# A graph-attention layer and a GCN layer on one core: other places for pieces of projections, the checks in layer 1, and the end in written order

## The chip, the core and the metric

The kernel runs on one NeuronCore of a Trainium2 chip. Five engines work in parallel, each on its own queue of instructions: TensorE (PE) multiplies matrices, VectorE (DVE) and ScalarE (ACT) compute elementwise, GpSimd (POOL) multiplies and copies, and SyncE (SP) here only issues DMAs. An engine takes its instructions in the order of its queue and stops at one whose semaphores have not come; whatever stands behind it waits too. The metric is the device time of one execution in microseconds (us).

## The reference

N = 2708 nodes with D = 128 features, H = 8 heads per feature. Layer 0 is an attention in which each of the 128 feature rows is a batch element of its own (the reshape cuts the N x 1024 projection so); layer 1 is a two-fold graph convolution with a dense `adj`:

```python
q = (x @ Wq.T).reshape(d, n, h)            # k, v alike; d = 128, h = 8
a = einsum('dnh,dmh->dnm', q, k) * d**-0.5 + adj + adj
a = softmax(a, axis=2)
x = layernorm(x + einsum('dnm,dmh->dnh', a, v).reshape(n, h*d) @ Wo.T)
lh = adj @ (x @ W2) + b2
e  = adj @ (lh @ W4) + b4 + lh @ res_w.T + res_b
x  = layernorm(x + e)
```

All in float32. The attention has 128 x 2708 x 2708 scores, so nearly all time is there.

## The kernel before, in words

**Startup.** `project_all` forms q, k and v of the first two 128-row chunks of x (L377) and stores them to DRAM. The other 20 chunks are projected in 240 "quarters" (chunk, one of q/k/v, a quarter of the columns) in between the attention's work. A quarter is one PE product (L344), a DVE copy (L346), for q and k two POOL instructions (L359, L360), stores (L364) and the load of the next quarter's weights `wc` (L336). `load_quarter(0)` (L407), which loads the first of these, stands on SP behind the stores of project_all.

**Attention.** The 128 feature rows are taken in 32 groups of 4. For each group, six blocks of 452 queries are worked through (the last 448). The keys are 22 chunks of 128 (the last has 20 rows). A block is nine steps, so there are 32 x 6 x 9 = 1728 steps. A step has two to four pieces; in a piece PE forms two tiles of scores in PSUM (L438) and DVE adds `adj` (L445). At the end of a step ACT takes the exponential of a tile `w` of three without `adj` (L534), which POOL multiplies by the exponential of `adj` (L535, `ecol`), and the exponential of the 4, 6 or 8 tiles `e` (L537). PE then adds the tiles up against the values (`add_up`, L455 to L463), at a block's end DVE copies the sums (`hand_on`, L469), and SP stores them to `os_` (L471). In group 0 `first_exp` (L418) forms the exponentials of `adj` and keeps them in DRAM; its `accum_out` gives their row sums for a check. `look_at_near` (L427) takes minima of the same columns in the last three groups.

**Order.** A planner, `interleave` (L40), writes the order of all this down ahead of time, from a cost for each operation; the engines keep that order. The quarters come in it as "amid": before the step numbers in the list `amid` (L474), so every 6 to 7 steps, up to step 1531. A quarter's further jobs (split, store, load) are issued one at a time at the second piece of the following steps.

**The end of layer 0.** After the attention SP loads seven weights (L544 to L550). `layer0_out` takes 22 chunks of 128 nodes: load `ot` (9 x 128 x 128, the sums with the divisor as the ninth row) and `xt`, two chunks ahead (L587, L589); reciprocal (L595); minimum and maximum of the divisor for a check (L598); multiply (L600); eight transposes on PE (L603), a copy by ACT (L605), the product with Wo (L611), the addition of x and its statistics on DVE (L615). After all chunks the normalisation and x @ W2 follow, four chunks at a time (L629 to L651), and a verdict over all checks (L652 to L667). If a check fails the program computes the attention again in a safer way (`tc.If`); this does not occur with these inputs.

**Layer 1.** Two passes of six column blocks (512 wide, the last 148). In each block 22 column tiles of `adjT` (256 KB each) are loaded by SP into 24 buffers (L679) and multiplied on PE (L680). Pass 1 gives `lhT` and from it `hw` (L691); pass 2 gives `eT` (L697), which is transposed (L700), added to x1 (L702), normalised (L577) and stored to `out` by SP (L705), 128 rows at a time. Layer 1 is not in written order: the framework's scheduler orders its instructions.

Of the kernel before, what the change touches and what calls it, by code (L numbers as in the profile page):

```python
# [18 lines left out]
P = 128  # L19
H = 8  # L20
# [10 lines left out]
NEAR_LOW = 1e-30  # L31
NEAR_HIGH = 1e18
# [110 lines left out]
def graph_attention_gcn(ctx: ExitStack, tc: tile.TileContext, x, xT, adj, adjT, adjP, adjS,  # L143
# [42 lines left out]
    ends = const.tile([P, 2, len(QBS) * len(TWO_EXP)], F32, name="ends")  # L186


    with ExitStack() as s:
# [184 lines left out]
        for n in range(2):  # L374
            load_adj(n)

# [30 lines left out]
        load_quarter(0)  # L407
# [5 lines left out]
        def first_exp(b, m):  # L413

            nw = QBS[b][1]
            t = ecols.tile([P, QB], F32, tag="ecol", name="ecol")
            x = b * len(TWO_EXP) + TWO_EXP.index(m)
            nc.scalar.activation(t[:, :nw], adj_cols[0, b, -1 - m][:, :nw], AF.Exp, scale=2.0,  # L418
                                 accum_out=ends[:, 1, x : x + 1])
            nc.sync.dma_start(near_exp[b, m][:, :nw], t[:, :nw])  # L420
            exp_cols[0, b, m] = t

        def look_at_near(g, b, m):

            x = TWO_EXP.index(m)
            if x % 3 == g - NG + 3:
                nc.vector.tensor_reduce(ends[:, 0, ds(b * len(TWO_EXP) + x, 1)], exp_cols[g, b, m][:, : QBS[b][1]],  # L427
                                        AX.X, ALU.min)
# [45 lines left out]
        amid = [2 + 32 * n // 5 for n in range(len(quarters))]  # L474
# [5 lines left out]
        for what, n, c, beside in interleave(plan, len(steps) // len(plan), NU, amid, bufs=5):  # L480
# [14 lines left out]
            if c == 1 and jobs:  # L495
                jobs.pop(0)()
            if c == 0:
# [34 lines left out]
            if c == len(pieces) - 1:  # L532
                look_at_near(g, b, two)
                nc.scalar.activation(w[:, :, :nw], sp[:, :, :nw], AF.Exp, scale=2.0)  # L534
                nc.gpsimd.tensor_mul(w[:, :, :nw], w[:, :, :nw],  # L535
                                     exp_cols[g, b, two][:, :nw].unsqueeze(1).to_broadcast([P, 3, nw]))
                nc.scalar.activation(e[:, :at, :nw], e[:, :at, :nw], AF.Exp, scale=2.0)  # L537
# [5 lines left out]
    wo = keep.tile([P, H, D], F32, name="wo")  # L543
    nc.sync.dma_start(wo.rearrange("g e f -> g (e f)"), WoT)  # L544
    w2, w4, rw = (keep.tile([P, P], F32, name=f"w{i}") for i in range(3))
    for t, src in ((w2, W2), (w4, W4), (rw, res_wT)):
        nc.sync.dma_start(t, src)
    b2_sb, b4_sb, rb_sb, bias = (keep.tile([P, 1], F32, name=f"b{i}") for i in range(4))
    for t, src in ((b2_sb, b2), (b4_sb, b4), (rb_sb, res_b)):
        nc.sync.dma_start(t, src)  # L550
    nc.vector.tensor_add(bias, b4_sb, rb_sb)

# [8 lines left out]
    reach = keep.tile([P, 2, NM], F32, name="reach")  # L561
    nc.gpsimd.memset(reach, 1.0)
    fine = keep.tile([P, 5], F32, name="fine")
# [6 lines left out]
    def layernorm(to, y, w):  # L570
        mv = stat.tile([P, nc.vector.BN_AGGR_DIM], F32, tag="mv", name="mv")
        statistics(mv[:w], y, w)
        sd = stat.tile([P, 1], F32, tag="sd", name="sd")
        nc.scalar.activation(sd[:w], mv[:w, 1:2], AF.Sqrt, bias=eps[:w])
        rs = stat.tile([P, 1], F32, tag="rs", name="rs")
        nc.vector.reciprocal(rs[:w], sd[:w])
        nc.vector.tensor_scalar(to, y, mv[:w, 0:1], rs[:w], ALU.subtract, ALU.mult)  # L577

    def layer0_out(sb, ps, pa, judge):
# [4 lines left out]
        def load(c):  # L584
            i0, w = MC[c]
            ot = sb.tile([P, H + 1, P], F32, tag="ot", name="ot")
            nc.sync.dma_start(ot[:w], o3[ds(i0, w)])  # L587
            xt = sb.tile([P, D], F32, tag="xt", name="xt")
# [3 lines left out]
        def divide(c):  # L592
# [3 lines left out]
            if judge:  # L596
                for i, op in enumerate((ALU.min, ALU.max)):
                    nc.vector.tensor_reduce(reach[:w, i, c : c + 1], ot[:w, H, :], AX.X, op)  # L598
            on = sb.tile([P, H, P], F32, tag="on", name="on")
            nc.vector.tensor_mul(on[:w], ot[:w, :H, :], rd[:w].unsqueeze(1).to_broadcast([w, H, P]))  # L600
# [16 lines left out]

        load(0)
        load(1)
        for c in range(NM + 2):  # L620
            if c + 2 < NM:
                load(c + 2)
            if c < NM:
                divide(c)
            if 0 <= c - 1 < NM:
                project(c - 1)
            if c >= 2:
                add_x(c - 2)
        sd, rs = (sb.tile([P, NM], F32, tag=n, name=n) for n in ("sds", "rss"))  # L629
        nc.scalar.activation(sd, mvs[:, :, 1], AF.Sqrt, bias=eps)  # L630
        nc.vector.reciprocal(rs, sd)
        for c0 in range(0, NM, 4):
            cs = range(c0, min(c0 + 4, NM))
            px = pa.tile([P, 4, P], F32, tag="px", name="px")
            x1T = sb.tile([P, 4, P], F32, tag="x1T", name="x1T")
            pw = pa.tile([P, 4, P], F32, tag="pw", name="pw")
            for c in cs:
                w = MC[c][1]
                nc.vector.tensor_scalar(x1[:w, c, :], ys[:w, c, :], mvs[:w, c, 0:1], rs[:w, c : c + 1],
                                        ALU.subtract, ALU.mult)  # L640
                nc.tensor.transpose(px[:, c - c0, :w], x1[:w, c, :], ident[:w, :w])

            full = len([c for c in cs if MC[c][1] == P])
            parts = [(0, full, P)] + [(c - c0, 1, MC[c][1]) for c in cs if MC[c][1] < P]
            for i, n, w in parts:
                nc.scalar.copy(x1T[:, ds(i, n), :w], px[:, ds(i, n), :w])
            for c in cs:
                w = MC[c][1]
                nc.tensor.matmul(pw[:w, c - c0, :], x1T[:, c - c0, :w], w2, start=True, stop=True)
            for i, n, w in parts:  # L650
                nc.scalar.copy(xw[:w, ds(c0 + i, n), :], pw[:w, ds(i, n), :])  # L651
        if judge:  # L652
            finite = sb.tile([P, NM * D], F32, tag="finite", name="finite", bufs=1)
            nc.vector.tensor_scalar(finite, ys.rearrange("p c f -> p (c f)"), 0.0, 0.0, ALU.mult, ALU.is_equal)
            nc.vector.tensor_reduce(fine[:, 0:1], finite, AX.X, ALU.min)
            bounds = [(reach[:, 0, :], ALU.min, SUM_LOW, ALU.is_ge), (reach[:, 1, :], ALU.max, SUM_HIGH, ALU.is_le)]
            bounds += [(ends[:, 0, :], ALU.min, NEAR_LOW, ALU.is_ge), (ends[:, 1, :], ALU.max, NEAR_HIGH, ALU.is_le)]
            for i, (a, way, limit, op) in enumerate(bounds):
                end = keep.tile([P, 1], F32, name=f"end{i}")
                nc.vector.tensor_reduce(end, a, AX.X, way)  # L660
                nc.vector.tensor_scalar(fine[:, 1 + i : 2 + i], end, limit, None, op)
            every, ones = (keep.tile([P, 1], F32, name=n) for n in ("every", "ones"))
            nc.vector.tensor_reduce(every, fine, AX.X, ALU.min)
            nc.gpsimd.memset(ones, 1.0)
            pf = pa.tile([P, NB], F32, tag="py", name="pf", bufs=2)
            nc.tensor.matmul(pf[:1, :1], every, ones, start=True, stop=True)
            nc.vector.tensor_copy(n_fine, pf[:1, :1])  # L667

    def layer1(s, cols):
# [4 lines left out]
        def propagate(src, n0, nw, last=None):  # L674

            acc = ps.tile([P, NB], F32, tag="wide", name="acc1")
            for m, (m0, mw) in enumerate(MC):
                t = cols.tile([P, NB], F32, tag="col", name="col1")
                nc.sync.dma_start(t[:mw, :nw], adjT[ds(m0, mw), ds(n0, nw)])  # L679
                nc.tensor.matmul(acc[:, :nw], src[:mw, m, :], t[:mw, :nw], start=(m == 0),  # L680
                                 stop=(last is None and m == NM - 1))
            if last is not None:
# [3 lines left out]
        for n0, nw in NBS:  # L686
            acc = propagate(xw, n0, nw)
            nc.vector.tensor_scalar(lhT[:, ds(n0, nw)], acc[:, :nw], b2_sb, None, ALU.add)
            for i, w in chunks(nw, P):
# [4 lines left out]
        for n0, nw in NBS:  # L694
            acc = propagate(hw, n0, nw, (rw, lhT[:, ds(n0, nw)]))
            eT = sb.tile([P, NB], F32, tag="eT", name="eT")
            nc.vector.tensor_scalar(eT[:, :nw], acc[:, :nw], bias, None, ALU.add)  # L697
            for i, w in chunks(nw, P):
                pe = pa.tile([P, NB], F32, tag="narrow", name="pe")
                nc.tensor.transpose(pe[:w, :D], eT[:, ds(i, w)], ident)  # L700
                y = sb.tile([P, D], F32, tag="y", name="y1")
                nc.vector.tensor_add(y[:w], pe[:w, :D], x1[:w, (n0 + i) // P, :])  # L702
                o = sb.tile([P, D], F32, tag="xo", name="xo")
                layernorm(o[:w], y[:w], w)
                nc.sync.dma_start(out[ds(n0 + i, w), :], o[:w])  # L705

    def rest(judge):
        with ExitStack() as s:
            cols = s.enter_context(tc.tile_pool(name="cols1", bufs=24))
            with ExitStack() as t:  # L710
# [3 lines left out]
                t.enter_context(tc.manual_schedule())  # L714
                layer0_out(sb, ps, pa, judge)
            layer1(s, cols)
# [136 lines left out]
```

## Time and profile before

| what | us |
|---|---|
| median of 3 runs (lowest, highest) | 6884.85 (6881.82, 6886.79) |
| profiled execution, its own time | 6884.26 |
| its span | 6882.5 |
| busy PE / DVE / ACT / POOL | 6655.3 / 6106.7 / 6505.4 / 5789.3 |
| last matmul of the attention ends | 6542.9 |
| first transpose of layer 0's end | 6555.6 |
| PE on layer 1 alone from | 6661.6 |
| last product of pass 2 starts | 6873.9 |

The span is from the first to the last instruction of the profiled execution; its own time has 1.8 us more around it. A busy share is an average over stages with different limits, so the stages have to be read on their own. A wait names what an engine waited for last; a wait of an engine that isn't the bottleneck of its stage costs nothing.

### The profile page before, as it was taken

What the parts mean: (1) busy time and instruction counts of PE and PEld (TensorE: products, weight loads), DVE (VectorE), ACT (ScalarE), POOL (GpSimd) and SP (SyncE); (2) the same over time, 40 slices, a digit from 0 to 9 for tenths busy, and PEclk for the clock granted to TensorE, in tenths of its full rate; (3) what the DMA queues carried; (4) which work ended last, traced back from release to release, by engine and by line L of the source; (5) the groups of instructions that cost most, each with busy time, mean ns of one, the idle gap of its engine ahead of it and who ended that gap; (6) DMA issues with size and microseconds to landing.
All of it is one profiled execution on the core that took longest, in us unless ns stands there. A gap on an engine that the chain in (4) does not pass through costs nothing.

```text
span 6882.5 us, 138849 instructions
## 1 busy us (share of the span) xinstructions
PE 6655.3 (97%) x50666; PEld 2002.7 (29%) x50666; DVE 6106.7 (89%) x6373; ACT 6505.4 (95%) x3659; POOL 5789.3 (84%) x2706
## 2 busy tenths in 40 slices
PE   7999999999999999999999999999999999999979
PEld 2222222222222222222222222222222222222254
DVE  6899999999999999999999999999999999999941
ACT  7999999999999999999999999999999999999910
POOL 5899988989888899998889999889898898888800
PEclk8999999999999999999999999999999999999999
DMA  8888888778888877788887778887788878777667
GB/s 254 261 250 250 249 244 248 243 246 250 249 254 245 239 245 244 246 251 252 246 243 248 244 240 250 242 253 243 248 251 247 249 233 239 243 233 230 193 204 233
DMA packets 1168590, 1674.27 MB, mean 243 GB/s; under 512 B 153982, under 2 KB 1135954, under 8 KB 1163802
## 3 DMA queue, kind: packets, MB, share of 16 engines
q1 hardware_dynamic: 1167642, 1664.50, 79.0%
q8 instruction: 402, 6.59, 0.4%
q14 instruction: 290, 2.38, 0.1%
q10 hardware_dynamic: 256, 0.81, 0.1%
HBM read 1582.90 MB, written 81.80 MB: 242 GB/s over the span
## 4 chain that ended last, share of the span: by engine, by line
PE 58%; DMA 11%; DVE 11%; POOL 6%; issue 5%; ACT 5%; SPq 4%; DVEq 0%; ACTq 0%; POOLq 0%
PE acc L463 29%; PE s L438 18%; DVE e L445 10%; POOL w L535 6%; DMA col<-in_adjP 4%; PE acc L680 3%; DMA two<-in_adjP 3%; ACT e L537 3%; PE p L438 2%; PE acc L455 2%; SPq L287 2%; ACT w L534 2%; DMA ecol<-ne 2%; PE s L344 1%; PE acc L460 1%
## 5 line engine op out<-in xcount | busy, mean ns | idle before, releaser
L535 POOL TENSOR_TENSOR w<-w,ecol 128x1356 f32<-128x1356 f32 (+1 forms) x1728 | 5347.8, 3102 | 696.1 <-ACT w L534 601.6
L445 DVE TENSOR_TENSOR e<-s,col 128x904 f32<-128x904 f32 (+1 forms) x4608 | 4817.2, 1091 | 320.6 <-PE s L438 130.3
L537 ACT ACTIVATE e<-e 128x2712 f32<-128x2712 f32 (+5 forms) x1728 | 4593.8, 2658 | 9.3 <-DVE e L445 4.3
L463 PE MATMUL acc<-e,vals 128*9 128x452 f32 x20352 | 3561.9, 545 | 0.4 <-ACT e L537 0.4
L438 PE MATMUL s<-q,k 32*128 32x452 f32 x10944 | 2475.2, 462 | 120.9 <-DVE e L445 93.3
L534 ACT ACTIVATE w<-p 128x1356 f32<-128x1356 f32 (+1 forms) x1728 | 2286.0, 1323 | 33.9 <-PE p L438 20.4
L438 PEld LDWEIGHTS s<-q,k 32*128 32x128 f32 x10944 | 997.6, 182 | 3267.6 <-DVE e L445 2845.5
L463 PE MATMUL acc<-w,vals 128*9 128x452 f32 x10368 | 1622.0, 544 | 0.0
L438 PE MATMUL p<-q,k 32*128 32x452 f32 (+1 forms) x5184 | 1328.1, 444 | 21.2 <-ACT w L534 19.6
L445 DVE TENSOR_TENSOR e<-s,two 128x904 f32<-128x904 f32 (+1 forms) x960 | 1048.3, 1092 | 126.5 <-PE s L438 81.3
L463 PEld LDWEIGHTS acc<-e,vals 128*9 128x9 f32 x20352 | 441.7, 88 | 786.2 <-issue 773.7
L438 PEld LDWEIGHTS p<-q,k 32*128 32x128 f32 x5184 | 547.1, 182 | 51.0 <-ACT w L534 45.3
L463 PEld LDWEIGHTS acc<-w,vals 128*9 128x9 f32 x10368 | 207.0, 88 | 175.8 <-issue 160.3
L262 POOL CAST k<-k_raw 128x336 fp32r<-128x336 f32 x251 | 222.2, 886 | 30.1 <-DMA q<-qs 30.1
L460 PE MATMUL acc<-e,v_first 128*32 128x452 f32 (+1 forms) x1536 | 188.9, 564 | 9.8 <-DVE o L469 2.0
L455 PE MATMUL acc<-e,v_short 128*128 128x452 f32 (+1 forms) x384 | 195.1, 590 | 0.0
L344 PE MATMUL s<-wc,xc 128*128 128x256 f32 (+1 forms) x480 | 166.4, 428 | 8.9 <-DMA wc<-in_WkT 7.5
L469 DVE COPY o<-acc 128x452 f32<-128x452 f32 x192 | 119.9, 624 | 40.0 <-PE acc L463 39.8
L360 POOL TENSOR_TENSOR pr<-pa,pr 128x256 fp32r<-128x256 f32 (+1 forms) x160 | 117.8, 736 | 12.8
L346 DVE TENSOR_SCALAR pa<-s 128x256 f32<-128x256 f32 (+1 forms) x240 | 100.2, 418 | 27.6 <-PE s L344 23.9
L344 PEld LDWEIGHTS s<-wc,xc 128*128 128x128 f32 (+1 forms) x480 | 70.5, 184 | 133.4 <-DVE e L445 116.4
L680 PE MATMUL acc<-col,xw 128*128 128x512 f32 (+2 forms) x264 | 106.0, 551 | 0.0
(85 smaller groups left out, 1041.6 us busy)
## 6 DMA issues: line engine op xcount, KB each, us to landing
col<-in_adjP SPq DMA_DIRECT2D x1965, 226.0 KB
two<-in_adjP SPq DMA_DIRECT2D x1440, 226.0 KB
ecol<-ne SPq DMA_DIRECT2D x1395, 226.0 KB
col<-in_adjP SPq DMA_DIRECT2D x393, 224.0 KB
two<-in_adjP SPq DMA_DIRECT2D x288, 224.0 KB
ecol<-ne SPq DMA_DIRECT2D x279, 224.0 KB
col<-in_adjT SPq DMA_DIRECT2D x210, 256.0 KB
k_raw<-ks SPq DMA_DIRECT2D x504, 84.6 KB
```

Of the source, the lines that this page charges most:

```text
L262: copy(k[:, :, ts(i, n)], t[:, ts(i, n * NU)].rearrange("p (q c) -> p c q", c=NU))
L287: queues[i].dma_start(q[ds(32 * j + 2 * H * i, 2 * H), :nw].bitcast(F32), qs[:, ds((GB * g + j) * N + n0, nw)])
L344: nc.tensor.matmul(pp[:mi, 0, :QW], given[c][:, :mi], given.pop((c, i, h)), start=True, stop=True)
L438: nc.tensor.matmul(to[:, :nw], k[r, m, :], q[r], start=True, stop=True)
L445: nc.vector.tensor_add(e[:, ds(at, 2), :nw], st[:, :, :nw], a)
L455: nc.tensor.matmul(a[:, :nw], vz, e[:, t, :nw], start=False, stop=False)
L460: nc.tensor.matmul(a[ds(32 * j, 32), :nw], v_first[g % 2][:, ds(32 * j, 32)], e[:, t, :nw], start=True, stop=False)
L463: nc.tensor.matmul(a[ds(32 * j, VW), :nw], v[:, m, ds(VW * j, VW)], e[:, t, :nw], start=False, stop=(m == last_chunk))
L534: nc.scalar.activation(w[:, :, :nw], sp[:, :, :nw], AF.Exp, scale=2.0)
L535: nc.gpsimd.tensor_mul(w[:, :, :nw], w[:, :, :nw], exp_cols[g, b, two][:, :nw].unsqueeze(1).to_broadcast([P, 3, nw]))
L537: nc.scalar.activation(e[:, :at, :nw], e[:, :at, :nw], AF.Exp, scale=2.0)
L680: nc.tensor.matmul(acc[:, :nw], src[:mw, m, :], t[:mw, :nw], start=(m == 0), stop=(last is None and m == NM - 1))
```

## The change

- **Startup and amid.** `load_quarter(0)` is issued before project_all. The amid pieces stand in front of steps 1, 4 and 8 of two blocks in turn: step numbers 8, 13, 19, 26, 31, 37 and so on up to 1441, the residues 8, 13 and 1 of 18 (13 is the step 4 of the second block of a pair).
- **Checks.** `accum_out` and `look_at_near` are gone, and so are minimum and maximum of the divisor in `divide`. Instead each of the 132 column tiles of pass 1 gets a maximum of absolute values on DVE, and `verdict` reads the divisors in one load of 1.39 MB; it runs in pass 2.
- **Weights.** Five of the weight loads are issued 40 steps before the end of the attention; the other two behind the first loads of `ot`.
- **Layer 0's end.** `ot` has four and `xt` six buffers in place of three each, and loads run three chunks ahead. POOL multiplies heads 5 to 7, DVE heads 0 to 4. Normalisation and x @ W2 of four chunks run inside the loop, one stage in each following turn.
- **Layer 1.** It is in written order now. What a block leaves to do (`form_hw` or `put_out`) is put on a list `due` and runs ahead of column 3 or 6 of a later block. `put_out` takes four chunks together and stores them with one DMA, on SP as before.

```diff
-    ends = const.tile([P, 2, len(QBS) * len(TWO_EXP)], F32, name="ends")
+    ends = const.tile([P, len(NBS) * NM], F32, name="ends")
...
+    def load_weights():
+        nc.sync.dma_start(wo.rearrange("g e f -> g (e f)"), WoT)
+        for t, src in ((w2, W2), (b2_sb, b2), (b4_sb, b4), (rb_sb, res_b)):
+            nc.sync.dma_start(t, src)
...
             load_adj(n)
+        load_quarter(0)
...
             project_all(1, i)()
-        load_quarter(0)
...
-            nc.scalar.activation(t[:, :nw], adj_cols[0, b, -1 - m][:, :nw], AF.Exp, scale=2.0,
-                                 accum_out=ends[:, 1, x : x + 1])
+            nc.scalar.activation(t[:, :nw], adj_cols[0, b, -1 - m][:, :nw], AF.Exp, scale=2.0)
...
-        amid = [2 + 32 * n // 5 for n in range(len(quarters))]
+        amid = [18 * (n // 3) + (1, 8, 13)[n % 3] for n in range(1, len(quarters) + 1)]
...
+            if n == len(steps) - 40 and c == 0:
+                load_weights()
...
-                look_at_near(g, b, two)
...
-            if judge:
-                for i, op in enumerate((ALU.min, ALU.max)):
-                    nc.vector.tensor_reduce(reach[:w, i, c : c + 1], ot[:w, H, :], AX.X, op)
             on = sb.tile([P, H, P], F32, tag="on", name="on")
-            nc.vector.tensor_mul(on[:w], ot[:w, :H, :], rd[:w].unsqueeze(1).to_broadcast([w, H, P]))
+            for multiply, e, n in ((nc.gpsimd.tensor_mul, 5, 3), (nc.vector.tensor_mul, 0, 5)):
+                multiply(on[:w, ds(e, n), :], ot[:w, ds(e, n), :], rd[:w].unsqueeze(1).to_broadcast([w, n, P]))
...
+        for c in range(NM + 4):
+            if c + 3 < NM:
+                load(c + 3)
             if c < NM:
                 divide(c)
             if 0 <= c - 1 < NM:
                 project(c - 1)
-            if c >= 2:
+            if stage2:
+                form_xw(*stage2)
+                stage2 = None
+            if 0 <= c - 2 < NM:
                 add_x(c - 2)
...
+            if stage1:
+                stage2 = stage1[0], normalise(*stage1)
+                stage1 = None
+            if c - 2 in steps_of:
+                stage1 = steps_of[c - 2], deviations(steps_of[c - 2])
...
+                if m in (3, 6) and due:
+                    due.pop(0)()
                 nc.tensor.matmul(acc[:, :nw], src[:mw, m, :], t[:mw, :nw], start=(m == 0),
                                  stop=(last is None and m == NM - 1))
+                if look:
+                    x = n0 // NB * NM + m
+                    nc.vector.tensor_reduce(ends[:mw, x : x + 1], t[:mw, :nw], AX.X, ALU.max, apply_absolute_value=True)
...
         for n0, nw in NBS:
-            acc = propagate(hw, n0, nw, (rw, lhT[:, ds(n0, nw)]))
+            acc = propagate(xw, n0, nw, look=judge)
+            take_lh(acc, n0, nw)
+            due.append(lambda n0=n0, nw=nw: form_hw(n0, nw))
+        if judge:
+            due.append(lambda: due.append(verdict(sb, pa)))
...
+        def put_out(eT, n0, nw):
...
+            for i, (at, x) in enumerate(chunks(nw, P)):
+                nc.tensor.transpose(pe[:x, i, :], eT[:, ds(at, x)], ident)
...
+            for i, k, x in parts:
+                nc.vector.tensor_add(y[:x, ds(i, k), :], pe[:x, ds(i, k), :], x1[:x, ds(c0 + i, k), :])
...
+            for i, k, x in parts:
+                nc.sync.dma_start(out[ds(n0 + i * P, k * x), :].rearrange("(c p) f -> p c f", p=x), o[:x, ds(i, k), :])
...
+        for n0, nw in NBS:
+            acc = propagate(hw, n0, nw, (rw, lhT[:, ds(n0, nw)]))
+            eT = take_e(acc, n0, nw)
+            due.append(lambda eT=eT, n0=n0, nw=nw: put_out(eT, n0, nw))
+        while due:
+            due.pop(0)()
...
+            s.enter_context(tc.manual_schedule())
```

## The prediction, on record before the changed kernel ran

> **What bounds the kernel now.** I read the page's busy shares first, then busy time by stage, then the groups with their idle time, and last the timelines at the two ends. The page and the stage windows (start:end, length, busy PE, PEld, DVE, ACT, POOL with instruction counts, PE clock, DMA share, GB/s):
>
> ```profile
> PE 6655.3 (97%) x50666; PEld 2002.7 (29%) x50666; DVE 6106.7 (89%) x6373; ACT 6505.4 (95%) x3659; POOL 5789.3 (84%) x2706
> ```
>
> ```profile
> 310.00:6540.00 6230.00, 6101.59 (x47690) 1751.91 (x47692) 5772.54 (x5838) 6197.51 (x3334) 5572.97 (x2572) 1.00 0.80 244
> 6543.00:6650.00 107.00, 71.83 (x545) 67.14 (x546) 74.46 (x180) 24.75 (x27) 0.41 (x5) 0.88 0.67 195
> 6650.00:6770.00 120.00, 120.00 (x372) 59.70 (x371) 10.06 (x19) 10.05 (x34) 0.00 (x0) 0.99 0.75 231
> 6770.00:6874.00 104.00, 104.00 (x284) 48.06 (x283) 22.44 (x105) 5.42 (x20) 0.00 (x0) 1.00 0.76 253
> ```
>
> The whole-span share names PE, the stages do not. In the attention ACT is busy 6197.5 of 6230 us, more than PE: the exponentials set the pace. In the 107 us of layer 0's end nobody is full. In both halves of layer 1 PE is busy all the time. The groups (busy, mean ns, then idle before them and its releaser) agree:
>
> ```profile
> L537 ACT ACTIVATE e<-e 128x2712 f32<-128x2712 f32 (+5 forms) x1728 | 4593.8, 2658 | 9.3 <-DVE e L445 4.3
> L534 ACT ACTIVATE w<-p 128x1356 f32<-128x1356 f32 (+1 forms) x1728 | 2286.0, 1323 | 33.9 <-PE p L438 20.4
> L344 PE MATMUL s<-wc,xc 128*128 128x256 f32 (+1 forms) x480 | 166.4, 428 | 8.9 <-DMA wc<-in_WkT 7.5
> ```
>
> Measured from end to end of the L537 instructions, an undisturbed block of nine steps takes 33.395 us. Over steps 60 to 1545 the excess is about 40 us, all beside the 240 amid pieces; once these are done it is near 0. The third line's 7.5 us is one wait in the startup. Its timeline, and SyncE's near the end of pass 2:
>
> ```profile
> 50.57 1.24 SPq L336 DMA_DIRECT2D wc<-in_WkT  x1
> 54.91 1.19 PE L344 MATMUL s<-wc,xc 128*128 128x256 f32 x2 [7.48 <-DMA wc<-in_WkT]
> ```
>
> ```profile
> 6830.35 1.51 SPq L705 DMA_DIRECT2D out<-xo  x3
> 6831.95 0.75 SPq L679 DMA_DIRECT2D col<-in_adjT  x2
> 6832.79 0.38 SPq L705 DMA_DIRECT2D out<-xo  x1
> 6833.26 13.11 SPq L679 DMA_DIRECT2D col<-in_adjT  x21
> ```
>
> SP does wait at the stores of `out` already (its waits between 6780 and 6883 us: 12.7 + 10.3 + 7.9 us on DVE), yet PE loses nothing, because the automatic schedule puts these stores some 20 loads ahead of what PE needs next.
>
> **What the Trainium skill says.** "DMA: Bandwidth & Descriptors", Anatomy of one DMA: a semaphore wait of a DMA happens on the issuing sequencer, before dispatch, and a DMA has about 2 us of fixed cost. The trace agrees: SP stands at L705, and a lone 256 KB column took 2.2 us from issue to landing (6654.09 to 6656.29). "TensorE: Matmul & The Clock Gate", HAM oscillation: a wait for DMA longer than some 3.4 us drops PE to half clock, and the next work starts cold. The trace: 0.5 from 6546.4 to 6560.1, behind PE's idle time from 6542.7 to 6555.6. "SBUF — State Buffer", Who interferes with whom: a VectorE instruction with two SBUF inputs and a GpSimd one that reads SBUF exclude each other. The trace doesn't show this pair; in the attention L445 has one PSUM input, and POOL's L535 runs steadily at 3.1 us beside it.
>
> **The change part by part.** The sum is against the profiled execution, 6884.26 us (span 6882.5, 1.8 us outside it); the median of the runs, 6884.85, is 0.6 us more.
>
> 1. Startup. `load_quarter(0)` goes from behind the stores of project_all to before them, so wc is there when PE asks. Step 1 took 8.1 us too long. PE is at half clock until 61 us, so some of it may come back: between 3 and 8, I take +5.5.
>
> 2. Group 0's exponentials lose their accumulator read: 54 x 0.09 us (start to start) on ACT, the bound: +4.9 (3 to 6).
>
> 3. Amid positions. 240 pieces go from every 6 to 7 steps to residues 1, 8 and 4 of each 18 steps (gaps 7, 5, 6). In the planner's order this is one 18-step pattern, repeated about 79 times. Its surroundings occur in the order before, too: a piece ahead of a 1 cost 0.00 us there, ahead of an 8 about 0.19, ahead of a 4 about 0.08. So 0.27 x 80 = 21 us, against 40: +19. Not seen before is a 4 only five steps behind an 8. At five places of before, in other surroundings, a 4 cost 0.41 to 0.55. From -5 to +24.
>
> 4. The 54 reduces L427 (0.61 us each, DVE, last three groups) vanish beside ACT: +1.5 (0 to 2). The five weight loads at step 1688 are 5 x 0.45 = 2.2 us of SP in a stage bound by ACT, with eight loads ahead: 0; without that cover 2.2.
>
> 5. Layer 0's end. Before, 4 stores and 7 loads stand on SP ahead of the first `ot` (6543.6 to 6548.3), which lands at 6552.9; PE starts at 6555.6. In the new order `ot` 0 stands ahead of the last `os` stores and the weights are long loaded: PE starts at about 6549. A chunk took 3.87 us (22 chunks, 85 us), paced by rd .95, two reduces, the multiply 1.22 and loads only two ahead. Now the reduces (0.41 x 2) are gone, loads run three ahead, and the multiply is split 5 : 3. POOL's share is an estimate: 3102 ns / 1356 x 384 = 0.88 us. PE needs 16 x 0.14 + the transposes, 2.8 us a chunk; with the DVE hand-over some 3.35 to 3.6. So PE is through at 6549 + 22 x 3.5 = 6626. The tail shrinks to the last two chunks' normalisation and x@W2, 5 to 10 us: layer 1 starts at about 6636. Before, PE was layer 1's alone from 6661.56 with 5 tiles done (5 x 0.877): effectively 6657.1. +21 (12 to 28). The lower end has the exclusion of DVE and POOL in it.
>
> 6. Pass 1 of layer 1: 132 reduces on DVE of 0.67 us (estimate, from L697's 0.75 for 128x512) under a column time of 0.877: hidden. Dearer than 0.877, each would hold its buffer back. The verdict's DVE work, some 12 us, has block 0 of pass 2 (19 us) to hide in: 0.
>
> 7. Pass 2. In written order a block's `out` store stands on SP between the column loads m=3 and m=4 of the next block (m=6 and 7 for block 0, behind the register load of n_fine). So the 24 buffers no longer help: SP can't issue column 4 before the block's normalisation is done. Counted from the last matmul of the block: PE does m=0 to 2 (3 x 0.877 = 2.63), four transposes (0.65), m=3, and has nothing more at 4.1. DVE: add of 128x512 (0.68), 4 x (0.24 + 0.17) statistics, ACT's root 0.29, reciprocal 0.16, 4 x 0.28 to scale, with hops 4.36, until 7.65. Then 0.475 us for the store's issue and 2.2 for the column's landing, up to 0.9 more behind the store's bytes: PE stands 6.2 to 7.1 us. Queued behind the store are all the later columns, and PE waits for each. Four such places x 6.7 = 27; block 5 (148 wide) has the same 6.7 plus 18 loads at SP's 0.475 against PE's 0.28, 3.5: 10. After each of five stalls one window of half clock, 3.4 / 2 = 1.6: 8. Together -45 (-35 to -55).
>
> Sum: 5.5 + 4.9 + 19 + 1.5 + 21 - 45 = 6.9 us less: 6877.4, as a median 6878.
>
> **The rivals.**
> (a) The stall in pass 2 is cheaper: the DVE chain is shorter, or the clock does not fall. With 4.5 us a place and 7 in block 5 it costs 25, not 45: 6857, faster. For it: no row shows the batched chain, and only a fully idle window halves the clock. Against it: the order on SP is fixed.
> (b) Slower: the piece at residue 4, five steps behind the one at 8, finds no slack on ACT and costs what it cost in odd surroundings, 0.43 to 0.55 instead of 0.08. 80 x 0.41 = 33 us lost: 6910. It decides once that piece costs over 0.34 us (then the sum is 14 worse than before). For it: those five places. Against it: in its usual surroundings the same local order cost 0.08.
> (c) DVE's and POOL's multiplies take turns (0.75 + 0.9 in place of 1.22, and rd behind it): 0.7 us a chunk, 15 us of item 5: 6892.
> (d) The excess belongs to a piece, not to its position: item 3 is 0 and the time 6896. Against it: 0.00 ahead of a 1.
>
> **How the numbers follow.** A measurement of this kernel tells about 0.2%, 14 us, from no change: under 6871 is faster, over 6898.6 slower. Forecast case 0.45 (6866 to 6890 for itself), (a) 0.2, (b) 0.15, (c) 0.12, (d) 0.08. Faster: 0.18 from (a), 0.12 from the good end of the forecast: 0.30. Slower: 0.13 from (b), 0.07 from bad ends of the rest: 0.20. Same: 0.50. The range reaches into (a) and nearly to (b): 6854 to 6902.
>
> **What the new profile would show.** Startup: no wait of PE at L344 for wc. Attention: end at about 6512 rather than 6543; the ends of the exponentials show what a piece ahead of 1, 4 and 8 costs. Layer 0's end: first transpose about 6 us after attention's last matmul, chunks of 3.35 to 3.6 us, POOL and DVE multiplies side by side or in turn. Pass 2: five idle times of PE, each ended by a column load behind a store of `out`, some 6 us long, and PE clock 0.5 behind each. The forecast is wrong if these are absent or twice as long, or if the blocks of the attention keep their excess.

## The result

The changed kernel takes 6898.5 us (median of 15 runs, 6892.7 to 6908.2), the kernel before 6886.0 (15 runs, 6881.8 to 6893.0). The ratio is 1.0018, 95% interval 1.0011 to 1.0025: 12.6 us slower, where 7 us less were forecast. The time lies in the stated range (6854 to 6902) and within 0.2% of before, but on the other side of it.

The profiled execution of the changed kernel has a span of 6905.8 us, 23.3 more than that of before, and is one of its longer executions (6907.55 us by itself); I use it for where the time lies, and medians for how much. Its page, part 1:

```profile
PE 6660.1 (96%) x50666; PEld 2005.2 (29%) x50666; DVE 6144.7 (89%) x6380; ACT 6498.6 (94%) x3595; POOL 5824.8 (84%) x2728
```

The stage windows after the change (columns as before: start:end, length, busy PE, PEld, DVE, ACT, POOL, PE clock, DMA share, GB/s). They are the attention, layer 0's end, pass 1 and pass 2:

```profile
310.00:6530.00 6220.00, 6085.56 (x47677) 1750.55 (x47672) 5751.16 (x5787) 6197.05 (x3334) 5573.89 (x2571) 1.00 0.81 244
6536.00:6623.60 87.60, 74.55 (x595) 68.51 (x595) 62.65 (x143) 30.36 (x41) 35.03 (x23) 0.93 0.79 231
6623.60:6735.20 111.60, 110.88 (x306) 52.42 (x305) 71.63 (x134) 5.25 (x22) 0.00 (x0) 0.98 0.76 227
6735.20:6897.00 161.80, 126.37 (x302) 56.78 (x301) 33.16 (x86) 2.01 (x7) 0.00 (x0) 0.86 0.54 186
```

Before, PE was busy all through both passes. Now pass 2 takes 162 us with PE busy for 126 and a clock of 0.86. What PE waits for in layer 1, by the waits from 6623 us on (us in total, times, longest), and the first of these places in the timeline:

```profile
PE acc L701 <- DMA col<-in_adjT: 35.2, 6, 7.0
```

```profile
6765.49 1.11 DVE L752 TENSOR_SCALAR xo<-y,mv,rs 128x128 f32<-128x128 f32 x4
6766.63 0.40 SPq L754 DMA_DIRECT2D out<-xo  x1
6767.14 3.81 SPq L698 DMA_DIRECT2D col<-in_adjT  x8
6770.18 1.22 PE L701 MATMUL acc<-col,hw 128*128 128x512 f32 x1 [6.99 <-DMA col<-in_adjT]
```

Read it downwards: DVE's last scaling, at once the store that waited for it on SP, 0.5 us later the first column load, and 3 us after that the PE, which had stood for 6.99 us. The other blocks give 6.75, 6.80, 6.87 and 6.81. Behind each, PE runs at half clock for 3.5 us and below full clock for as long again (0.67 to 0.83 at the five places). Here are the two windows behind the first stall:

```profile
6770.00:6773.50 3.50, 3.32 (x4) 1.51 (x5) 0.00 (x0) 0.00 (x0) 0.00 (x0) 0.50 1.03 368
6773.50:6777.00 3.50, 3.50 (x7) 1.49 (x6) 0.00 (x0) 0.00 (x0) 0.00 (x0) 0.71 1.04 392
```

The 23.3 us between the two profiles, cut at the same places. The attention's rows come from the ends of the e exponentials in the timeline; the excess is what the steps took beyond the pace of the undisturbed block, 33.395 us for nine. Layer 1's effective start before is 6657.1, as in the prediction.

| stretch | before, us | after, us | gain |
|---|---|---|---|
| first e exponential ends | 49.6 | 55.1 | -5.5 |
| excess of steps 0 to 59 | 38.0 | 35.3 | +2.7 |
| excess of steps 60 to 1545 (amid) | 38.6 | 34.6 | +4 |
| excess of the rest | 6.9 | 0.9 | +6 |
| last e exponential to layer 1 | 116.9 | 90.6 | +26.3 |
| pass 1 | 107.1 | 111.6 | -4.5 |
| pass 2 | 110.2 | 162.2 | -52 |
| after the last product | 8.1 | 8.4 | -0.3 |

The first row is these two instructions (start, length), before and after:

```profile
46.34 3.22 ACT L537 ACTIVATE e<-e 128x3616 f32<-128x3616 f32 x1 [0.93 <-DVE e L445]
```

```profile
51.86 3.22 ACT L541 ACTIVATE e<-e 128x3616 f32<-128x3616 f32 x1 [0.93 <-DVE e L446]
```

In the changed kernel PE no longer waits for wc in the startup. From 45 to 90 us these waits for columns stand there instead:

```profile
DVE e L446 <- DMA col<-in_adjP: 4.5, 2, 4.1
ACT ecol L427 <- DMA col<-in_adjP: 4.4, 2, 3.7
```

### The profile page after: what moved, and what is told of

The parts are those of the page before. It is cut to its first block, busy times and chain, and to the rows that moved or that the text cites. A ratio compares the mean times of both kernels' runs of the same rounds, so it can differ in the third digit from the quotient of the medians.

```text
span 6905.8 us, 138828 instructions
## 1 busy us (share of the span) xinstructions
PE 6660.1 (96%) x50666; PEld 2005.2 (29%) x50666; DVE 6144.7 (89%) x6380; ACT 6498.6 (94%) x3595; POOL 5824.8 (84%) x2728
## 4 chain that ended last, share of the span: by engine, by line
PE 52%; DMA 12%; DVE 10%; ACT 7%; issue 7%; POOL 6%; SPq 6%; DVEq 0%; POOLq 0%; ACTq 0%
PE acc L464 25%; PE s L439 16%; DVE e L446 9%; POOL w L539 5%; ACT e L541 4%; DMA col<-in_adjP 4%; ACT w L538 3%; SPq L297 3%; PE acc L701 3%; DMA two<-in_adjP 2%; PE p L439 2%; DMA ecol<-ne 2%; PE acc L456 2%; PE s L354 1%; DMA k_raw<-ks 1%
## 5 line engine op out<-in xcount | busy, mean ns | idle before, releaser
L541 ACT ACTIVATE e<-e 128x2712 f32<-128x2712 f32 (+5 forms) x1728 | 4706.5, 2724 | 22.7 <-DVE e L446 17.5
L538 ACT ACTIVATE w<-p 128x1356 f32<-128x1356 f32 (+1 forms) x1728 | 2399.7, 1389 | 7.3 <-PE p L439 5.6
L701 PE MATMUL acc<-col,hw 128*128 128x512 f32 (+2 forms) x264 | 119.8, 605 | 35.3 <-DMA col<-in_adjT 35.2
```

## The experiments

**The store on another queue.** As the changed kernel, one word different:

```diff
-                nc.sync.dma_start(out[ds(n0 + i * P, k * x), :].rearrange("(c p) f -> p c f", p=x), o[:x, ds(i, k), :])
+                nc.scalar.dma_start(out[ds(n0 + i * P, k * x), :].rearrange("(c p) f -> p c f", p=x), o[:x, ds(i, k), :])
```

> The changed kernel with the store of `out` issued by ACT instead of SP. Theory: the wait of that store at the head of SP's queue holds back the column loads; each of five places costs PE some 6.9 us of idle time and the half clock after it. Then PE does not stand in pass 2, layer 1 takes about 226 us as before the change instead of 282, and the median falls by 50 to 55 us to about 6846. Rival: the columns would come late anyway (landing time, bandwidth behind the store's 256 KB); then PE still stands several us in each block and the median stays above 6885.

6849.4 us (6845.2 to 6854.4), ratio to before 0.995, 0.9933 to 0.9967: 49 us less than the changed kernel, and faster than both. Its two passes as windows, and all that PE waited for from 6724 to 6836:

```profile
6613.20:6724.40 111.20, 110.49 (x305) 52.26 (x304) 71.46 (x134) 5.25 (x22) 0.00 (x0) 0.98 0.76 230
6724.40:6835.00 110.60, 110.51 (x303) 51.18 (x302) 33.16 (x86) 2.01 (x7) 0.00 (x0) 1.00 0.78 269
```

```profile
PE pe L740 <- DVE eT L728: 0.5, 1, 0.5
```

Pass 2 is back at 110.6 us with the same normalisation and the same bytes; no column is late. The rival (columns late anyway) falls. ACT bears the wait at no cost, since nothing on its queue is due in that time: ahead of one block's root it stands idle for 17.6 us, and the store comes right behind that root. What the Trainium skill says in "DMA: Bandwidth & Descriptors" (Anatomy of one DMA), that a DMA's semaphore wait happens on the issuing sequencer, is just what decides here: 49 us by the choice of the sequencer.

**The half clock alone.** The store stays on SP; behind the column matmul that follows put_out's transposes stand seven matmuls whose result nobody reads:

```diff
+        def keep_busy():
+            t = pw.tile([P, NB], F32, tag="busy", name="busy")
+            for i in range(7):
+                nc.tensor.matmul(t, hw[:, 0, :], lhT[:, :NB], start=True, stop=True)
...
                                  stop=(last is None and m == NM - 1))
+                while warm:
+                    warm.pop(0)()
...
                 nc.tensor.transpose(pe[:x, i, :], eT[:, ds(at, x)], ident)
+            warm.append(keep_busy)
```

> The changed kernel with its store on SP, and seven matmuls of 128x512 whose result nobody reads behind the column matmul that follows each put_out's transposes; they fill 6.1 us of PE's idle time in pass 2. The stalls stay, only the half clock after them should go. Theory: the half clock costs the 13.8 us by which PE's busy time on the columns of pass 2 grew (119.8 against 106): 6885. Rival: the stall is all of it and the half clock costs little: 6898 or slower by the extra matmuls.

6891.7 us (6884.1 to 6896.7), 6.8 less than the changed kernel. Pass 2 from the end of its first block, first the changed kernel, then this one:

```profile
6755.00:6897.00 142.00, 106.57 (x254) 48.28 (x253) 21.59 (x76) 1.49 (x5) 0.00 (x0) 0.84 0.48 164
```

```profile
6752.00:6884.00 132.00, 125.87 (x325) 56.39 (x323) 21.96 (x77) 1.49 (x5) 0.00 (x0) 0.99 0.52 177
```

The clock goes from 0.84 to 0.99 and the stretch from 142 to 132 us, so the half clock is a cost of its own (as the Trainium skill has it in "TensorE: Matmul & The Clock Gate", HAM oscillation): 7 us by the medians, 10 by the profiles. The expectation of 13.8 us set PE's busy time on the columns of pass 2 against 106. The groups before and after the change say 104.1 and 119.8, so it had grown by 15.7:

```profile
L680 PE MATMUL acc<-col,hw 128*128 128x512 f32 (+2 forms) x264 | 104.1, 545 | 0.0
```

```profile
L701 PE MATMUL acc<-col,hw 128*128 128x512 f32 (+2 forms) x264 | 119.8, 605 | 35.3 <-DMA col<-in_adjT 35.2
```

In this run it is 109.5. Most of the 5.4 us that don't come back lie in the last, narrow block:

```profile
6874.85 7.88 PE L703 MATMUL acc<-col,hw 128*128 128x148 f32 x34 [0.19 <-DMA col<-in_adjT]
```

These 17 columns took 0.46 us each, about the rate at which SP issues them (18 in 8.74 us). In the run with the store on ACT, where they had been loaded ahead, a column took 0.27 us (19 in 5.14). So at full clock PE catches up with columns that SP can only now issue, and part of what the half clock cost is lost to that.

**Written order for layer 0's end only.** The manual schedule moves inward; layer 1's code stays:

```diff
-            s.enter_context(tc.manual_schedule())
...
+                t.enter_context(tc.manual_schedule())
                 layer0_out(sb, ps, pa)
```

> The changed kernel with written order for layer 0's end only; layer 1, same code, goes back to the framework's scheduler, which in the build puts the stores of a block 18 to 25 column loads later on SP. Theory: the written order is what makes the stall; without it as fast as e1_out_act, 6849 within 5. Rival: one store of 256 KB for four chunks, waiting for the slowest of them, is what stalls SP: above 6880.

6857.9 us (6847.4 to 6864.5), 0.9956 of before. The profile shows no wait of PE from 6735 to 6850, and in SP's timeline the stores stand a block later:

```profile
6770.85 13.22 SPq L698 DMA_DIRECT2D col<-in_adjT  x22
6788.24 0.40 SPq L754 DMA_DIRECT2D out<-xo  x1
6788.73 17.60 SPq L698 DMA_DIRECT2D col<-in_adjT  x25
```

SP still waits at a store, but with 14 to 23 columns issued beyond the one PE works on. So neither the batch of four chunks nor the single store is at fault, only the place that the written order gives it. It is 8.5 us above the run with the store on ACT, more than the 5 expected; in its one profile the attention's excess is 34.8 us (25.0 there), and the ranges of the 4 runs each overlap.

**The positions alone, in the kernel before.**

```diff
-        amid = [2 + 32 * n // 5 for n in range(len(quarters))]
+        amid = [18 * (n // 3) + (1, 8, 13)[n % 3] for n in range(1, len(quarters) + 1)]
```

> The kernel before with the new list amid alone. Theory from the trace after the change: the pieces' excess on ACT over steps 60 to 1545 stays near 35 us (38 in the kernel before), since a piece ahead of 8 costs 0.3 to 0.4; the wait for wc at step 1 (8 us) goes because the first piece stands at step 8: about 10 us faster than before, 6875. Rival, the forecast's term: excess 21 us, 27 us faster, 6859.

6871.9 us (6865.6 to 6874.7), 0.9978 (0.9968 to 0.9989): 13.9 less than before. Excess of steps 60 to 1545: 28.7 us. The wait for wc is gone, as the first piece now stands at step 8, and yet the start-up has hardly gained: steps 0 to 53, less what every step of group 0 has (0.56), lose 6.3 us instead of 7.4. The waits from 45 to 90 us show what has come in its place, the next columns:

```profile
ACT ecol L418 <- DMA col<-in_adjP: 4.1, 3, 3.2
DVE e L445 <- DMA col<-in_adjP: 3.8, 2, 3.1
```

**The old positions in the fast kernel.** The store on ACT, and the list `amid` of before:

> As e1_out_act, with the old amid list (every 6 to 7 steps) and the early load of wc kept, so that only the positions differ. Theory: the excess is 38 us instead of 25 to 28: 11 us slower than e1_out_act, 6860. The forecast's term would make it 19: 6868. Rival: the positions do nothing and what e3_before_amid gained was the wait for wc alone: 6849.

6865.8 us (6863.2 to 6871.3): 16.4 more than with the new positions. Excess of steps 60 to 1545: 47.4 us against 25.0. So the positions are worth 14 us (in the kernel before) to 16 us, the startup included in both. The excess with the new ones scatters between executions, 24.1 to 34.8 in nine profiles with these positions and otherwise the same attention; the changed kernel's own profile, 34.6, is near the top. That is why the table above shows only 4.

**Load of wc back in its old place**, in the changed kernel:

```diff
             load_adj(n)
-        load_quarter(0)
...
             project_all(1, i)()
+        load_quarter(0)
```

> The changed kernel with load_quarter(0) back behind the stores of project_all. Theory: the two early loads push the startup's 16 key loads back (SP issued its eight from 16.75 to 31.85 us instead of 16.5 to 28.1), and the first exponential of e ended at 55.1 us instead of 49.6; with the load back it ends near 49.6, no piece waits for wc because the first stands at step 8 now, and the median falls by about 6 us. Rival: the start differs from execution to execution by as much, and the median stays within 2 us.

6896.2 us (6891.7 to 6904.6), 2.3 less, inside the scatter. The first e exponential ends at 53.8 us, so the theory falls: SP's eight key loads took 14.0 us here, 15.1 in the changed kernel, 12.5 and 11.6 in the two kernels on the base of before. All profiles on the base of the change end the first e at 53.1 to 55.1, the two on the old base at 49.6 and 51.8. This 2 to 5 us is unexplained: the order on SP of this run is the same as before's down to the first steps.

**The multiply wholly on DVE**, in the changed kernel:

```diff
-            for multiply, e, n in ((nc.gpsimd.tensor_mul, 5, 3), (nc.vector.tensor_mul, 0, 5)):
+            for multiply, e, n in ((nc.vector.tensor_mul, 0, 8),):
```

> The changed kernel with the multiply of layer 0's end wholly on DVE (1.22 us) instead of 0.82 us on DVE and 1.6 us on POOL. Theory: PE sets the pace now (transposes 1.04 and products 1.95, 2.95 us a chunk); with all of it on DVE, DVE has 0.95 + 1.22 + 0.29 + 0.29 + 0.18 and a share of the normalisation, 3.3 us with gaps, and sets it: 22 x 0.35 = 8 us slower than the changed kernel. Rival: DVE and POOL hold each other up over SBUF, and without POOL the chunks take 2.95 us still or less: no difference, within 2 us.

6899.1 us (6894.0 to 6907.4): no difference. From the first transpose to the last, 21 chunks took 71.6 us (3.41 each) against 71.2 (3.39). PE's own work is 1.04 + 1.95 a chunk and a quarter of 0.60 + 1.06 for the folded normalisation, 3.40: it sets the pace either way (busy 64.2 of 71.1 us here, 66.5 of 70.7 in the changed kernel). The time is the rival's; whether DVE and POOL hold each other up needed two more runs.

**POOL five heads, DVE three**; and **the second reciprocal in PSUM**:

```diff
-            for multiply, e, n in ((nc.gpsimd.tensor_mul, 5, 3), (nc.vector.tensor_mul, 0, 5)):
+            for multiply, e, n in ((nc.gpsimd.tensor_mul, 3, 5), (nc.vector.tensor_mul, 0, 3)):
```

> The changed kernel with POOL multiplying five heads (640 elements) and DVE three (384) in layer 0's end. DVE's 640 took 0.82 us and POOL's 384, started 0.05 us later, 1.6 us. Theory: they take turns; POOL's instruction is 0.82 us of waiting and about 0.8 of work (L539's rate, 3.1 us / 1356, gives 0.88): POOL then takes 0.5 + 1.4 = 1.9 to 2.0 us. Rival: POOL is slow on this shape, 4.2 ns an element: 2.7 us.

```diff
+            rp = pa.tile([P, P], F32, tag="rp", name="rp")
+            nc.vector.reciprocal(rp[:w], ot[:w, H, :])
+            for multiply, r, e, n in ((nc.gpsimd.tensor_mul, rd, 5, 3), (nc.vector.tensor_mul, rp, 0, 5)):
+                multiply(on[:w, ds(e, n), :], ot[:w, ds(e, n), :], r[:w].unsqueeze(1).to_broadcast([w, n, P]))
...
-            made[c] = pa.tile([P, NB], F32, tag="py", name="py", bufs=2)
+            made[c] = pa.tile([P, NB], F32, tag="py", name="py", bufs=1)
```

> The changed kernel with DVE forming the reciprocal a second time into PSUM (one more 0.95 us per chunk, and one PSUM buffer of the product with Wo given up for it), and its multiply reading that: no VectorE instruction beside POOL's multiply has two SBUF inputs any more. Theory: POOL's 384 elements then take 0.8 to 0.9 us instead of 1.6. Rival: POOL's rate is what it is: 1.6. The time of the whole is not what is asked; with the extra reciprocal it should be some 15 to 25 us longer.

POOL's multiply by shape (busy, mean ns, idle before), in the changed kernel, with five heads, and with PSUM:

```profile
L585 POOL TENSOR_TENSOR on<-ot,rd 128x384 f32<-128x384 f32 x21 | 33.4, 1592 | 40.2 <-DVE rd L581 33.9 <-PE pt L588 5.4 <-DMA col<-in_adjT 0.9
```

```profile
L585 POOL TENSOR_TENSOR on<-ot,rd 128x640 f32<-128x640 f32 x21 | 39.2, 1865 | 37.4 <-DVE rd L581 25.4 <-PE pt L588 8.3 <-PE px L622 3.2
```

```profile
L587 POOL TENSOR_TENSOR on<-ot,rd 128x384 f32<-128x384 f32 x21 | 21.0, 998 | 58.1 <-DVE rd L581 52.3 <-PE py L598 3.6 <-DMA col<-in_adjT 2.3
```

Two thirds more elements cost POOL only 0.27 us more, as DVE's instruction beside it got shorter by about as much (0.825 to 0.558): close to the theory's 1.9 us, far from the rival's 2.7. With the second reciprocal the same 384 elements take 1.00 us instead of 1.59. There, however, POOL's multiply ran mostly beside DVE's reciprocal into PSUM (in one chunk POOL from 6572.52 to 6573.52, the reciprocal from 6572.31 to 6573.21) and met DVE's multiply (from 6573.24) only for its last 0.3 us. So that run shows that 1.59 us is not POOL's own rate; that reading PSUM is what frees it, it doesn't show by itself. Both runs fit the turns that DVE and POOL take while both of DVE's operands lie in SBUF, as the Trainium skill says in "SBUF — State Buffer" (Who interferes with whom). There is one run of each (6896.1 and 6909.7 us); the second, with its extra reciprocal, is 11 us above the changed kernel's median, less than the 15 to 25 expected.

**A piece ahead of 6, or of 7, instead of 8**, both with the store on ACT:

```diff
-        amid = [18 * (n // 3) + (1, 8, 13)[n % 3] for n in range(1, len(quarters) + 1)]
+        amid = [18 * (n // 3) + (1, 6, 13)[n % 3] for n in range(1, len(quarters) + 1)]
```

> As e1_out_act (the store on ACT's queue, 6849), with the amid pieces at residues 1, 6, 13 of 18 instead of 1, 8, 13, so the piece ahead of step 8 stands ahead of step 6. Theory: what a piece costs ACT is set by DVE's slack in the steps behind it; a piece ahead of 8 meets the hand-on copy and the four-piece step 0, and costs 0.26 to 0.31; one ahead of 6 cost 0.15 in the kernel before. Then the excess over steps 60 to 1545 falls from some 27 us to about 15, and the median to about 6838. Rival: a piece costs the same wherever it stands, or the cost moves to the others as the gaps change: 6849 within 3.

7034.0 us (7010 to 7055), 185 slower than with the piece ahead of 8, and neither theory nor rival had it. The excess is 210.7 us. PE's waits over the attention:

```profile
PE s L354 <- DMA wc<-in_WkT: 44.9, 20, 4.6
PE s L354 <- DMA wc<-in_WqT: 43.0, 20, 3.9
```

and SP's timeline ahead of one such place, where the piece's matmul started at 3577.33:

```profile
3556.57 0.33 SPq L313 DMA_DIRECT2D col<-in_adjP  x1
3564.24 1.21 SPq L374 DMA_DIRECT2D qs<-pr  x2
3565.54 1.41 SPq L472 DMA_DIRECT2D os<-o  x4
3567.05 3.77 SPq L297 DMA_DIRECT2D q<-qs  x8
...
3572.80 0.38 SPq L346 DMA_DIRECT2D wc<-in_WqT  x1
```

SP stood from 3556.9 to 3564.2 for the piece ahead of 1 to be split by POOL, then issued the sums' stores and eight loads of q, and only then the weights for the piece ahead of 6. With five steps between them the load comes late: the same mechanism as in pass 2, a wait at the head of SP's queue. These waits make 88 us; the rest came with them (a mean clock of 0.979 against 0.994), and I did not take that apart. One step more (7 instead of 6):

> As e1_out_act, with amid at 1, 7, 13 of 18: the piece that cost 185 us ahead of step 6 (five steps behind the one ahead of 1) stands one step later. In e5_amid_1_6_4 that piece waited for wc 2.2 us on average, 4.6 at most, because on SP its load stood behind the wait of the hand-on's os store and eight loads of q. Theory: one step is 3.5 us, so that wait all but goes, and what is left is what a piece ahead of 7 cost in the kernel before, 0.33, as much as one ahead of 8: 6849 to 6855. Rival: what was dear in e5_amid_1_6_4 is the place behind the hand-on, not the gap of five steps: well above 6880.

6865.4 us (6863.8 to 6866.7). No wait for wc is left, so the gap was what was dear at 6. But a piece ahead of 7 costs 0.56 us there, not the 0.33 of the kernel before (excess 45.8 against 25.0), mostly by ACT's waits for PE:

```profile
ACT w L538 <- PE p L439: 34.4, 68, 3.3
```

With the piece ahead of 8 that group is 3.3 us. So 8 was better than 6 or 7, by one set of runs each.

## Why the prediction was wrong

The largest term, the stall in pass 2, was foreseen with its cause and its place. But the sum of +6.9 us is a difference of large terms, and items 1, 3, 6 and 7 were all set too favourably, item 1 by the most.

- **Item 1, startup (+5.5): this step failed.** It priced the wait that goes and put at nothing what would be late next. The wait for wc went, and waits for columns took its place: steps 0 to 53 lose 6.3 to 13.5 us to waits in every profile but the one at 6 (7.4 in the kernel before). On top, the first exponential came 3.5 to 5.5 us later in kernels on the base of the change, for a reason left open; the early load of wc is not it, by the run that took it back. Together, on the base of the change with the positions 1, 8, 4 or 1, 7, 4, the startup came out 4.5 to 8 us worse than in the one profile of before (with the positions alone, in the kernel before, 1 us worse), where 5.5 better was forecast. That is 10 to 14 us, against 19.5 us between forecast and result.
- **Item 2, the accumulator reads (+4.9): right.** Group 0's steps went from 0.56 to 0.47 us above the base, 54 x 0.09.
- **Item 3, positions (+19): mechanism right, size too high.** 14 to 16 us by medians. A piece ahead of 1 and 4 cost what was said (0 and 0.06 to 0.09), one ahead of 8 cost 0.25 to 0.30 plus up to 0.10 two steps before, where 0.19 had been read from few places. Rival (b), the 4 five steps behind the 8, fell; rival (d), positions don't matter, fell with the runs at 6 and 7. In the changed kernel's own profile the blocks did keep most of their excess, a sign of being wrong that the prediction had named: the attention's last sums were there at 6535.7, not at about 6512.
- **Item 4 (+1.5):** the last steps gained 6 in the profile, but not by the reduces as far as the profiles show: the run with the positions alone keeps them and has an excess of about 3 there, the kernels without them have 1 to 4.
- **Item 5, layer 0's end (+21): right, at the good end of its range.** First transpose 6.6 us after the attention's last sums were there (6535.7 to 6542.3), chunks of 3.39 us, 26.3 us in all. Rival (c) was right that DVE and POOL take turns and wrong that it matters: PE sets the pace.
- **Item 6, pass 1 (0): -4.5.** The reduces are hidden (0.61 us each under 0.877), and PE stands idle for only 0.7 us. But the first 20.4 us of the pass ran at a clock of 0.87, an estimate of 2.7 us lost (20.4 x 0.13); the rest was not taken apart.
- **Item 7, pass 2 (-45): mechanism, place and stall right** (6.2 to 7.1 us forecast, 6.75 to 6.99 found). Pass 2 lost 52 us in the profile and 49 by the run with the store on ACT. PE's waits for columns came to 35.2 us, where 37 had been priced. What was short is the half clock: priced at 8 us, as 3.4 / 2 for each of five stalls (1.7, not the 1.6 written there), while the clock behind the stalls gives an estimated 2.3 to 2.9 us each (the first: 3.5 x 0.50 + 3.5 x 0.29), and PE's busy time on the columns grew by 15.7 us. Rival (a), a cheap stall, fell.

Taken together, by medians: positions +14 to +16, store -49, and the rest must be +20 to +22 to give -12.6. The forecast had 19, -45 and +33 for the same three.

## What to carry to other kernels

A prefetch is only as deep as its queue is free of waits: 24 buffers were worth nothing behind one store that waited for its data, and moving that store to a queue with nothing due (ACT here) gave 49 us. When an order is written out by hand, ask of each DMA that waits what stands behind it on the same queue, and who needs that within the wait. And when a stall is removed, look for the next arrival in line before counting it as gain; where a forecast is the difference of large terms, state its sign with no more confidence than the weakest of them allows.

## What was not expected of the hardware

After a stall of 6.9 us on PE with SP held up, keeping PE busy brought the clock back from 0.84 to 0.99 but only 7 to 10 us of the 15.7 by which PE's busy time on the columns had grown. And a projection piece one or two steps earlier (of 3.7 us each) changed the time of the whole kernel by 16 and 185 us.
